# Third pass of a scan, attention and feed-forward kernel: the second y half added by a DMA, y normalized on GpSimd

## The chip, the cores and the metric

The kernel runs on one core of a Trainium2 chip. The metric is the device time of one execution in microseconds (us). The engines are named as the profile names them: PE (TensorE, with PEld for its weight loads), DVE (VectorE), ACT (ScalarE), POOL (GpSimd) and SP (SyncE, which here only issues DMAs). A DMA can be issued from SP's, ACT's or POOL's queue.

## What is computed

Eight images of 64x64 tokens with 96 channels go through two layers. The first is a selective scan in four directions (rows and columns, forwards and backwards), whose four results are added, normalized over 192 channels, gated and projected back to 96 channels. The second is linear attention and a quantized feed-forward block, each behind a layer normalization.

```python
x = x + _L0_conv_ref(_gn(x), ...)
#   y = out_y[:, 0] + inv_y[:, 0] + wh_y + invwh_y          # four directions
#   y = (y - mu) * rsqrt(var + 1e-05) * ln_gamma + ln_beta  # over 192 channels
#   out = (y * silu(z)) @ out_proj_w.T
t = _to_tokens(x)
t = t + _L1_attn_ref(_ln_t(t), ...)      # no softmax: q (k^T v)
t = t + _L1_ffn_ref(_ln_t(t), ...)       # fp8 products, relu, fp8 products
```

## The kernel before

The kernel has three passes. `pass1` normalizes, projects and convolves; `pass2` runs the scans and takes most of the time; `pass3` does everything from the sum of the directions to the output. The change lies in `pass3` alone.

`pass2` leaves two arrays per image in memory, `y_d[b][0]` (the two row directions, added) and `y_d[b][1]` (the two column directions, added), each of 4096 tokens by 192 channels in fp32. `pass3` works on units of 512 tokens (`GRP`), eight per image (`UNITS`), 64 in all. A unit is held as a tile of 128 partitions by 4 groups of tokens (`NU`).

For each unit there are three generators:

- `load(b, q)` (L1139): SP issues five DMAs: `y` and `yo` (the two halves, 384 KB each), two for `zs` (the gate), and `xr` (the residual input). There are five buffers of each (`LOADED`, slots "loaded").
- `first_part(b, q)` (L1154): POOL adds `yo` to `y` (L1162). `standardize` (L1121) takes DVE's statistics of `y` (four `bn_stats`, four `bn_aggr`), ACT's square root, DVE's reciprocal and product, and then four ACT activations, which write the normalized `y` in place (L1137). PE transposes `y`, ACT scales by gamma and beta into `gt`, POOL multiplies `gt` by `zs` (L1179, twice per unit), PE projects, DVE adds the residual into `t`, `t` is standardized into `ln`, and PE adds to the Gram matrix of the image and makes the transposed `lnT`.
- `second_part(b, q)` (L1241): after `attention(b)`, which needs all eight Gram contributions of the image: PE's product with `weff`, DVE's addition, a third standardization (`lf`), transposes, the quantized feed-forward block (with POOL's cast to `hq`, L1278, and POOL's two additions, L1290 and L1291), and the store of `t` by SP.

`fills()` (L1100) writes constants into the padding of `ln` and `lf` once, on POOL; `first_part` waits for it before the second standardization.

The order of instructions on each engine is fixed when the program is written. `weave` (L169) is a planner: each generator yields (engine, cost, delay, slots), and `weave` always takes the step that can begin first on its engine, by costs in us and delays that stand in the code; ties go by rank. First parts have their rank lowered by 12, so they come ahead of second parts. A generator can also yield a key and wait until `done` has it. `room` says how many generators of a kind are open at once: five first parts, five second parts and one load. The next load is opened when the one before has ended. `InOrder` (L85) then ties each engine's instructions to this order. So an instruction whose data is late holds back all that stand behind it on its engine, whatever the plan thought.

In a load, SP's step has a cost of 7.0 (0.0 for the first three units) and a delay of 2.5. It is the load's only step:

```python
end = yield "sp", 0.0 if b == 0 and q < EARLY else 7.0, 2.5, slots["loaded"]
```

Of the kernel before, what the change touches and what calls it, by code (L numbers as in the profile page):

```python
# [33 lines left out]
F32 = mybir.dt.float32  # L34
# [4 lines left out]
ALU = mybir.AluOpType  # L39
# [3 lines left out]
P = 128  # L43
NB, HH, WW, C = 8, 64, 64, 96
L = HH * WW
DI, N, R, K = 192, 16, 6, 4
# [975 lines left out]
def pass3(ctx, tc, g, ident, mhalf, engines, y_d, z_d, out):  # L1022
    nc = tc.nc
    pe, dve, act, pool = engines
    CA = C + 1
    sp = InOrder(tc, nc.sync)

    def pool_of(name, **kwargs):
        return ctx.enter_context(tc.tile_pool(name=f"p3{name}", reuse_waits="tile", bufs=1, **kwargs))

    OPEN = 5
    NU = GRP // P
    UNITS = L // GRP
    LOADED, HELD, EARLY = 5, 20, 3
    first_w, loaded = pool_of("first"), pool_of("loaded")
    wp, one, each, gates, held = (pool_of(name) for name in ("w", "one", "each", "gates", "held"))
    two = ctx.enter_context(tc.tile_pool(name="p3two", reuse_waits="tile", bufs=2))
    banks = {"tr": 3, "mm": 2, "ph": 2}
    slots = {name: Buffers(count) for name, count in {**banks, "loaded": LOADED, "held": HELD, "gates": 3}.items()}
# [59 lines left out]

    def fills():  # L1100

        yield "added", 1
        end = yield "pool", 3.2
        for i in range(OPEN):
            pool.memset(lns[i][:, :, C:P], 0.0)
            pool.memset(lns[i][:, :, C:CA], 1.0)
        for i in range(OPEN):
            pool.memset(lfs[i][:, :, C:P], 0.0)
        done[("filled",)] = end

    done, counts = {}, {}
    loads, holds, grams, weffs = {}, {}, {}, {}

    def take(name, shape):
        which = slots[name].taken
        return pools[name].tile(shape, F32, name=name, tag=f"{name}{which}"), which

    def tokens(src, q):
        return src[q * GRP : (q + 1) * GRP].rearrange("(n p) c -> p n c", p=P)

    def standardize(src, dst, name, cost, which):  # L1121

        yield "dve", 4 * (cost - 0.18) + 0.27
        st = each.tile([P, NU, 6], F32, name=f"st{name}", tag=f"st{name}{which % OPEN}")
        mv = mvs[name][which % OPEN]
        for i in range(NU):
            dve.bn_stats(st[:, i, :], src[:, i, :])
        for i in range(NU):
            dve.bn_aggr(mv[:, i, 0:2], st[:, i, :])
        yield "act", 0.2, 0.2  # L1130
        act.activation(mv[:, :, 1], mv[:, :, 1], AF.Sqrt, bias=eps)
        yield "dve", 0.3, 0.2
        dve.reciprocal(mv[:, :, 1], mv[:, :, 1])
        dve.tensor_reduce(mv[:, :, 3], mv[:, :, 0:3], mybir.AxisListType.X, ALU.mult)
        yield "act", 4 * cost
        for i in range(NU):
            act.activation(dst[:, i, 0 : src.shape[2]], src[:, i, :], AF.Identity, bias=mv[:, i, 3:4], scale=mv[:, i, 1:2])  # L1137

    def load(b, q):  # L1139
        cols = slice(q * GRP, (q + 1) * GRP)  # L1140
        end = yield "sp", 0.0 if b == 0 and q < EARLY else 7.0, 2.5, slots["loaded"]
        of = slots["loaded"].taken
        y, yo = (loaded.tile([P, NU, DI], F32, name=name, tag=f"{name}{of}") for name in ("y", "yo"))
        for o, dst in enumerate((y, yo)):
            sp.dma_start(dst, tokens(y_d[b][o], q))
        zs = loaded.tile([P, 2, GRP], F32, name="zs", tag=f"zs{of}")
        sp.dma_start(zs[:, 0, :], z_d[b][0:P, cols])
        sp.dma_start(zs[:, 1, :], z_d[b][DI - P : DI, cols])
        xr = loaded.tile([P, NU, C], F32, name="xr", tag=f"xr{of}")
        sp.dma_start(xr, tokens(g["x"][b], q))  # L1150
        loads[b, q] = y, yo, zs, xr, of
        done["load", b, q] = end

    def first_part(b, q):  # L1154
        yield "load", b, q
        y, yo, zs, xr, of_loads = loads[b, q]
        end = yield "pool", 1.8, 0.2, slots["held"]
        of_hold = slots["held"].taken
        t = held.tile([P, NU, C], F32, name="t", tag=f"t{of_hold}")
        lnT = held.tile([P, GRP], F32, name="lnT", tag=f"lnT{of_hold}")  # L1160
        holds[b, q] = t, lnT, of_hold
        pool.tensor_add(y, y, yo)  # L1162
        done["added", b * UNITS + q] = end
        if b * UNITS + q < OPEN:
            yield ("gamma",)
        yield from standardize(y, y, "y", 0.44, b * UNITS + q)
        for i, ch in enumerate((slice(0, P), slice(DI - P, DI))):
            yield "pe", 0.6, 0.2, slots["tr"]
            pt, slot = take("tr", [P, GRP])
            for n in range(NU):  # L1170
                pe.transpose(pt[:, n * P : (n + 1) * P], y[:, n, ch], ident)
            end = yield ("act", 0.67) if i else ("act", 0.67, 0.2, slots["gates"])
            if i == 0:
                of_gt = slots["gates"].taken
                gt = gates.tile([P, 2, GRP], F32, name="gt", tag=f"gt{of_gt}")
            act.activation(gt[:, i, :], pt, AF.Identity, bias=gb[:, i, 1:2], scale=gb[:, i, 0:1])
            slots["tr"].release(slot, end)
            yield "pool", 1.23
            pool.tensor_mul(gt[:, i, :], gt[:, i, :], zs[:, i, :])  # L1179
        end = yield "pe", 1.7, 0.2, slots["mm"]  # L1180
        slots["gates"].release(of_gt, end)
        po, slot = take("mm", [P, NU, C])
        for i in range(NU):
            blk = slice(i * P, (i + 1) * P)
            pe.matmul(po[:, i, :], gt[:, 0, blk], w_out0, start=True, stop=False)
            pe.matmul(po[:, i, :], gt[:, 1, blk], w_out1, start=False, stop=True)
        end = yield "dve", 0.55, 0.0
        dve.tensor_add(t, po, xr)
        slots["mm"].release(slot, end)
        slots["loaded"].release(of_loads, end)  # L1190
        ln = lns[(b * UNITS + q) % OPEN]
        yield ("filled",)
        yield from standardize(t, ln, "t", 0.36, b * UNITS + q)
        if b > 0:
            yield "gram", b - 1
        end = yield "pe", 0.9
        if b not in grams:
            grams[b] = ps_one.tile([P, CA], F32, name="pg")
        counts["gram", b] = counts.get(("gram", b), 0) + 1
        for i in range(NU):  # L1200
            first, last = counts["gram", b] == 1 and i == 0, counts["gram", b] == UNITS and i == NU - 1
            pe.matmul(grams[b], ln[:, i, :], ln[:, i, 0:CA], start=first, stop=last)
        if counts["gram", b] == UNITS:
            done["grams", b] = end
        yield "pe", 0.7, 0.2, slots["tr"]
        pl, slot = take("tr", [P, GRP])
        for i in range(NU):
            pe.transpose(pl[:, i * P : (i + 1) * P], ln[:, i, :], ident)
        end = yield "act", 0.47
        act.copy(lnT, pl)  # L1210
        slots["tr"].release(slot, end)
# [29 lines left out]
    def second_part(b, q):  # L1241
# [11 lines left out]
        slots["mm"].release(slot, end)  # L1253
        lf = lfs[(b * UNITS + q) % OPEN]
        yield from standardize(t, lf, "f", 0.36, b * UNITS + q)

        yield "pe", 0.7, 0.2, slots["tr"]
# [36 lines left out]
        slots["held"].release(of_hold, end)  # L1294

    units = [("parameters", -20, parameters()), ("fills", -20, fills())]
    for b in range(NB):
        units += [("first", b * UNITS + q - 12, first_part(b, q)) for q in range(UNITS)]
        units += [("load", b * UNITS + q, load(b, q)) for q in range(UNITS)]
        units.append(("attention", 0, attention(b)))  # L1300
        units += [("second", b * UNITS + q, second_part(b, q)) for q in range(UNITS)]
# [46 lines left out]
```

## Time and profile before

| What | Value |
|---|---|
| time, median of 3 runs | 9698.91 us (9694.32 to 9705.02) |
| profiled execution: time, span | 9701.46 us, 9699.7 us |
| TensorE clock granted, mean | 0.978 |
| busy share of the span: PE, DVE, ACT, POOL | 82%, 96%, 94%, 92% |
| first sum of `y` and `yo` on POOL | begins at 9029.8 us |
| last sum of `y` and `yo` on POOL | begins at 9596.6 us |

The shares of the span are set by `pass2`, which takes most of it. `pass3` is about the last 690 us: its first load is issued at 9006.3 us. In a table of stretches, each row is one stretch of the span with the busy time and the number of instructions of each engine. A group row gives count, busy time and the mean duration of one, then the engine's idle time just before and what ended it. Nearly every instruction is recorded on one line of the code (L93, the helper `InOrder`), so groups are told apart by the names of the tiles they write and read. All `y` tiles of the three passes share the name `y` in the profile.

### The profile page before, as it was taken

Reading aid. Unit: us, or ns where it says so; the run is one execution under the profiler, and the core shown is the slowest. Engines: PE = TensorE matmul, PEld = TensorE weight load, DVE = VectorE, ACT = ScalarE, POOL = GpSimd, SP = SyncE. Lnnn points to the kernel's source line nnn. Section 1 sums busy time; section 2 is a strip of 40 time slices with the busy share of each in tenths; the row PEclk is TensorE's granted clock in tenths of the full one; section 3 lists DMA queues with packets and bytes.
Section 4 is the critical chain, followed back from the end, with each engine's and each line's share of the span. In section 5 each row is a group of like instructions: output and inputs, shape, how many; then the busy total and the mean of one; then the engine's idle time right before and its main releaser. Section 6 shows DMA issues by size and latency. Waiting matters only on the chain.

```text
span 9699.7 us, 163458 instructions
## 1 busy us (share of the span) xinstructions
PE 7931.9 (82%) x57287; PEld 6133.9 (63%) x57287; DVE 9295.1 (96%) x6986; ACT 9091.7 (94%) x21482; POOL 8951.6 (92%) x2903
## 2 busy tenths in 40 slices
PE   8768888888888888888888888888888888888787
PEld 4346666666666666666666666666666666666676
DVE  8989999999999999999999999999999999999688
ACT  6679999999999999999999999999999999999787
POOL 1449999999999999999999999999999999999787
PEclk9889999999999999999999999999999999999898
DMA  6777777799987776799977777899867767999763
GB/s 186 223 222 229 236 233 232 241 221 209 215 225 228 235 228 225 234 215 211 218 226 232 231 227 227 227 208 214 225 220 235 226 219 232 217 209 213 198 184 111
DMA packets 939733, 2120.78 MB, mean 219 GB/s; under 512 B 277707, under 2 KB 425964, under 8 KB 937378
## 3 DMA queue, kind: packets, MB, share of 16 engines
q1 hardware_dynamic: 932226, 2083.33, 77.8%
q10 hardware_dynamic: 6256, 26.05, 0.9%
q8 instruction: 458, 7.50, 0.3%
q14 instruction: 361, 2.96, 0.1%
q0 software_dynamic: 432, 0.94, 0.0%
HBM read 1934.36 MB, written 175.66 MB: 218 GB/s over the span
## 4 chain that ended last, share of the span: by engine, by line
ACT 21%; DVE 13%; issue 9%; POOL 6%; PE 4%; DMA 2%; SPq 0%; DVEq 0%; POOLq 0%; ACTq 0%
DVE h L93 10%; ACT x L93 9%; ACT da L93 7%; POOL c L93 5%; PE wide L93 2%; DVE wide L93 2%; PE acc L93 1%; DMA c<-xd_d 1%; ACT y L93 1%; ACT L93 1%; PE mm L93 1%; POOL xg L93 1%; ACT delta L93 1%; ACT duT L93 1%; ACT lf L93 0%
## 5 line engine op out<-in xcount | busy, mean ns | idle before, releaser
L93 POOL TENSOR_TENSOR c<-c,h 128x2048 f32<-128x2048 f32 x1536 | 6969.2, 4575 | 54.5 <-DVE h L93 38.7
L93 DVE TENSOR_TENSOR_SCAN h<-da,carry,wide 128x1024 f32<-128x1024 f32 x2304 | 5243.3, 2327 | 71.2 <-PE wide L93 33.2
L93 ACT ACTIVATE x<-duT,bT 128x128 f32<-128x128 f32 (+1 forms) x14336 | 4229.9, 368 | 2.1
L93 ACT ACTIVATE da<-delta,a_neg 128x1024 f32<-128x1024 f32 x3072 | 3503.8, 1145 | 178.2 <-DVE h L93 168.1
L93 PE MATMUL acc<-ident,c 128*128 128x128 f32 x24576 | 3126.1, 276 | 360.2 <-POOL c L93 349.1
L93 PEld LDWEIGHTS acc<-ident,c 128*128 128x128 f32 x24576 | 2754.7, 142 | 816.4 <-POOL c L93 703.7
L93 PE MATMUL wide<-ident,x 128*128 128x128 f32 x11264 | 1499.3, 277 | 401.1 <-DVE h L93 314.3
L93 DVE TENSOR_TENSOR_SCAN h<-da,wide 128x1024 f32<-128x1024 f32 x768 | 1704.3, 2267 | 41.5 <-PE wide L93 18.2
L93 PEld LDWEIGHTS wide<-ident,x 128*128 128x128 f32 x11264 | 1250.8, 142 | 662.3 <-ACT x L93 203.9
L93 DVE TENSOR_TENSOR wide<-du,wide 128x1024 f32<-128x1024 f32 x1216 | 1455.0, 1208 | 34.8 <-PE wide L93 31.4
L93 PE MATMUL acc<-sel,zero 96*128 96x512 bf16 x4135 | 1136.6, 380 | 0.0
L93 PE MATMUL wide<-xb,sel 96*128 96x512 bf16 x2432 | 720.4, 380 | 286.3 <-DVE h L93 250.2
L93 POOL TENSOR_TENSOR xg<-duT,bT 128x512 f32<-128x512 f32 (+1 forms) x640 | 901.3, 1428 | 8.1 <-ACT duT L93 8.0
L93 PE MATMUL wide<-ident,xg 128*128 128x128 f32 x3584 | 482.7, 278 | 168.4 <-DVE h L93 153.3
L93 PEld LDWEIGHTS <-zero 96*128 96x128 bf16 x4135 | 401.8, 98 | 320.0 <-issue 4.2
L93 PEld LDWEIGHTS wide<-ident,xg 128*128 128x128 f32 x3584 | 399.5, 143 | 261.6 <-issue 198.5
L93 PEld LDWEIGHTS <-sel 96*128 96x128 bf16 x2432 | 222.6, 98 | 477.3 <-issue 297.0
L93 POOL TENSOR_TENSOR du<-delta,u 128x1024 f32<-128x1024 f32 x192 | 460.9, 2400 | 28.6 <-DMA u<-u_d 25.4
L93 DVE SCALAR_TENSOR_TENSOR u<-xpad,conv_w,u 128x4096 f32<-128x4096 f32 (+1 forms) x104 | 448.3, 4310 | 2.2
L93 ACT ACT_TABLE_LOAD x197 | 252.8, 1283 | 29.4 <-DVE ut L93 13.8
L93 PE MATMUL wide<-ident,du 128*128 128x128 f32 x1536 | 204.8, 276 | 84.6 <-DVE h L93 71.7
L93 PE MATMUL px<-u,w_xp 128*128 128x512 f32 x448 | 225.6, 646 | 49.1 <-ACT u L93 30.3
(148 smaller groups left out, 6016.8 us busy)
## 6 DMA issues: line engine op xcount, KB each, us to landing
c<-xd_d SPq DMA_DIRECT2D x1024, 1024.0 KB
c<-xd_d SPq DMA_DIRECT2D x1024, 512.0 KB
u<-u_d SPq DMA_DIRECT2D x127, 512.0 KB
xdt<-dt_d SPq DMA_DIRECT2D x1146, 36.0 KB
xb<-b_d SPq DMA_DIRECT2D x382, 96.0 KB
u<-u_d SPq DMA_DIRECT2D x128, 256.0 KB
zs<-z_d SPq DMA_DIRECT2D x128, 256.0 KB
y_d<-y SPq DMA_DIRECT2D x96, 256.0 KB
```

Of the source, the lines that this page charges most:

```text
L93: ins = getattr(self.engine, op)(*args, **kwargs).ins
```

## The change

The tile `yo` and its load from SP's queue are gone. In its place POOL's queue issues a DMA that adds `y_d[b][1]` to `y` in SBUF as it lands. This is a second step of the load's generator, with a cost of 0.7 and a delay of 3.0, so a load ends there. POOL's sum is gone. The normalization of `y` is moved from ACT to POOL: four `tensor_scalar` instructions of 192 elements (multiply, then add, with a value per partition each), in one step with a cost of 1.3. `fills` waits for the second load in place of the second sum. The slot "held" is taken by DVE's statistics step instead of POOL's sum. The number of buffers is the same.

```diff
     def fills():
-        yield "added", 1
+        yield "load", 0, 1

     def standardize(src, dst, name, cost, which):
-        yield "dve", 4 * (cost - 0.18) + 0.27
+        if cost is not None:
+            yield "dve", 4 * (cost - 0.18) + 0.27
...
         dve.tensor_reduce(mv[:, :, 3], mv[:, :, 0:3], mybir.AxisListType.X, ALU.mult)
+        if cost is None:
+            yield "pool", 1.3
+            for i in range(NU):
+                pool.tensor_scalar(dst[:, i, :], src[:, i, :], mv[:, i, 1:2], mv[:, i, 3:4], ALU.mult, ALU.add)
+            return
         yield "act", 4 * cost

     def load(b, q):
...
-        y, yo = (loaded.tile([P, NU, DI], F32, name=name, tag=f"{name}{of}") for name in ("y", "yo"))
-        for o, dst in enumerate((y, yo)):
-            sp.dma_start(dst, tokens(y_d[b][o], q))
+        y = loaded.tile([P, NU, DI], F32, name="y", tag=f"y{of}")
+        sp.dma_start(y, tokens(y_d[b][0], q))
...
-        loads[b, q] = y, yo, zs, xr, of
+        loads[b, q] = y, zs, xr, of
+        end = yield "pool", 0.7, 3.0
+        pool.dma_start(y, tokens(y_d[b][1], q), accum_op=ALU.add)
         done["load", b, q] = end

     def first_part(b, q):
         yield "load", b, q
-        y, yo, zs, xr, of_loads = loads[b, q]
-        end = yield "pool", 1.8, 0.2, slots["held"]
+        y, zs, xr, of_loads = loads[b, q]
+        yield "dve", 4 * (0.44 - 0.18) + 0.27, 0.2, slots["held"]
...
-        pool.tensor_add(y, y, yo)
-        done["added", b * UNITS + q] = end
+        yield from standardize(y, y, "y", None, b * UNITS + q)
         if b * UNITS + q < OPEN:
             yield ("gamma",)
-        yield from standardize(y, y, "y", 0.44, b * UNITS + q)
```

## The prediction

> **What bounds the kernel now.** The change is confined to the third pass, so I cut that pass out first. The moments come from the timeline: the first sum of the two y halves starts at 9029.8 us, the last at 9596.6, the span ends at 9699.7. The table of stretches gives the load of the engines in the three stages that this makes (columns: stretch, length, busy time and count of PE, PEld, DVE, ACT, POOL, granted clock, DMA share, GB/s).
>
> ```profile
> 9030.00:9150.00 120.00, 84.59 (x536) 74.83 (x537) 63.62 (x361) 81.31 (x188) 64.32 (x58) 0.77 0.76 224
> 9150.00:9597.00 447.00, 375.57 (x3021) 323.83 (x3020) 383.76 (x1791) 404.54 (x1000) 354.95 (x285) 0.94 0.60 178
> 9597.00:9700.00 103.00, 73.52 (x558) 54.50 (x556) 73.41 (x299) 65.75 (x162) 62.51 (x57) 0.83 0.12 34
> ```
>
> The same table for the tile yo counts 16 sums in stage A (first row) and 48 in stage B. So a unit of 512 tokens costs 120/16 = 7.5 us in A, where no engine is full, and 447/48 = 9.31 us in B. In B, ACT is busy 8.43 us of it (90.5%), DVE 8.00, PE 7.82, POOL 7.39. ACT is the fullest, but DVE is close behind: if ACT shrinks, DVE allows little. The tail of 103 us holds no first parts and isn't touched.
>
> Next, the groups of ACT and POOL for what moves, and rows near to what is new on POOL (columns: count, busy us, mean ns of one, idle before).
>
> ```profile
> L93 ACT ACTIVATE y<-y,mvy 128x192 f32<-128x192 f32 x256 | 119.2, 543 | 17.0 <-DVE mvy L93 15.8 <-DVE mvt L93 1.0 <-DVE mvf L93 0.2
> ```
>
> ```profile
> L93 POOL TENSOR_TENSOR y<-y,yo 128x768 f32<-128x768 f32 x64 | 116.1, 1816 | 18.2 <-DMA yo<-y_d 18.2
> L93 POOL CAST hq<-h 128x1536 fp8e5<-128x1536 f16 x64 | 93.7, 1465 | 55.6 <-DVE h L93 47.1 <-PE ph L93 4.5 <-DMA zs<-z_d 1.8
> ...
> L93 POOL DMA_DIRECT2D xdt<-dt_d x6 | 3.2, 548 | 0.0
> ...
> L93 POOL DMA_DIRECT2D u<-u_d x1 | 0.6, 577 | 0.0
> ...
> masks.py:199 POOL TENSOR_SCALAR_AFFINE_SELECT ident<-ident 128x128 f32<-128x128 f32 x1 | 0.3, 288 | 0.0
> ```
>
> The loads' times to landing stand in the chain of waits (start, us, what) and, for POOL's queue, in the list of DMA issues (last number).
>
> ```profile
> 9037.09 4.13 DMA yo<-y_d
> ...
> 9053.36 4.00 DMA yo<-y_d
> ...
> 9070.17 7.49 DMA y<-y_d
> ...
> 9198.26 3.28 DMA y<-y_d
> ```
>
> ```profile
> u<-u_d POOLq DMA_DIRECT2D x1, 512.0 KB, 12.1
> ...
> xdt<-dt_d POOLq DMA_DIRECT2D x6, 36.0 KB, 8.2
> ```
>
> Last, DVE's timeline for one unit's statistics in B, from their start to the last reduction.
>
> ```profile
> 9296.25 1.13 DVE L93 BATCH_NORM_STATS2 sty<-y 128x6 f32<-128x192 f32 x4
> ...
> 9299.20 0.17 DVE L93 RECIPROCAL mvy<-mvy 128x4 f32<-128x4 f32 x1
> 9299.41 0.17 DVE L93 TENSOR_REDUCE mvy<-mvy 128x4 f32<-128x12 f32 x1
> ```
>
> That is 9299.58 - 9296.25 = 3.3 us, ACT's square root and its queue included. The same stretch in A, 9079.20 to 9081.40, takes 2.2 us.
>
> **The change part by part.** *Off ACT:* four normalizations, 119.2/64 = 1.86 us a unit; ACT falls to 6.6 us in B. Alone this is worth at most what DVE leaves: 63 us of DVE idle time in B.
>
> *On POOL:* the sum goes, 1.82 us. Four normalizations of 192 elements come, which no row shows. From below: the cast does 1536 elements in 1.465 us, so 768 take 0.73, plus three more starts of about 0.1 (the mean of the 128x4 memset): 1.0 us. From above: the two-input sum of 768 elements, 1.82, plus the same starts: 2.1. The one-input AFFINE_SELECT of 128 elements took 0.288; four of them with 1.5 times the elements are 1.15 to 1.73. It is nearest in kind; I take 1.4. The issue of the adding load: 0.548 to 0.577 us for 18 to 128 rows; this one has 512 runs of 768 bytes, so from 0.52 (the xb loads) to 4 x 0.577 = 2.3. Rows of 18 and 128 hardly differ, so 0.7. POOL in B: 7.39 - 1.82 + 0.7 + 1.4 = 7.7 us, not the bound; with both upper ends 10.0, and then it is.
>
> *SP* issues four loads a unit instead of five, about 0.5 us less of a queue that waits for buffers anyway: nothing. *DMA:* the bytes from memory are the same; the destination is read as well, on engines 60% busy in B: nothing but the landing time below. *DVE* keeps its work. *The memsets* of fills, 2.3 us on POOL, now wait for the second load instead of the second sum; POOL's waits of 9.7 and 3.8 us there hide them, without that they cost 2.3 us once.
>
> *The new wait.* The adding load waits on POOL for the first y load, and everything on POOL waits behind it. That y has one planned period of lead (7.0 + 2.5 us), against 3.3 to 7.5 to land, so this wait is nothing; in a burst, up to 7.5 once. The wait that costs is the next: DVE's statistics for the landing, and behind them all of DVE's queue.
>
> *What the order does.* The planner opens one load at a time (room 1). So far a load ended with SP's step, and the next could start at once. Now it ends with POOL's step, so the next load begins on SP no earlier than the adding load of this unit, and its own adding load comes at least 7.0 + 2.5 = 9.5 planned us later. In the plan the normalization of this unit follows its adding load by 0.7 + 3.0 + 1.61 + 0.4 + 0.5 = 6.2 us. So POOL's queue reads: adding load u, normalization u, adding load u+1. The queue is fixed, and on the chip it is a loop with one unit in it: landing, statistics, square root, reciprocal, normalization, next adding load. Its length is a floor for the period, and two-unit prefetch, which today lets five loads run ahead of the sum, no longer hides the second half.
>
> Landing time L, from POOL's issue: below, the fastest row of the same 384 KB, 3.28; above, POOL's own transfers, 12.1. Its twin yo took 4.0 to 4.1, y in a burst 7.5. The adding load also reads its destination and starts beside the next unit's y, zs and xr loads. I take 5.0. The loop in B: 5.0 + 3.3 + 1.4 + 0.2 (two releases) = 9.9; in A: 5.0 + 2.2 + 1.4 + 0.2 = 8.8.
>
> Sum: A 16 x (8.8 - 7.5) = +21; B 48 x (9.9 - 9.31) = +28; the first unit waits 5.0 instead of 1.8, +3. Together +52 on the profiled execution's 9701.5 us, which is 2.5 above the median of the runs: 9751, so 9750. The loop is level with today at L = 4.2 (64 L = 48 x 4.41 + 16 x 3.7).
>
> The Trainium skill, "DMA: Bandwidth & Descriptors", section "Anatomy of one DMA — SWDGE (gpsimd) path", gives a POOL-issued transfer about 2.0 us plus its bytes at 436 GB/s; as an estimate 2.9 us here. The loads above took longer than that, but by it the loop would be 7.8 us and the change a gain of the second rival's size.
>
> A second rule speaks against the change, and a row bears on it.
>
> ```profile
> L93 DVE TENSOR_SCALAR h<-h,b1q x144: 319/346/1909, 9153.0 to 9599.5; 128x512 f16<-128x512 f16 x144
> ```
>
> DVE's bias step on h takes 346 ns in the median and up to 1909 (columns minimum/median/maximum). The Trainium skill, "SBUF — State Buffer", section "Who interferes with whom", says that such an operation and GpSimd lock each other out of a shared port pair, and a descriptor write waits too. Three medians, 1.0 us, before an issue would make L 6.0 and the sum about 64 us more; shorter POOL instructions would, by the same rule, give DVE some back.
>
> **The rivals.** *1, the other side: ACT's relief comes through.* If L stays below 4.2, the loop is shorter than today's period and DVE becomes the bound. For it: yo's 4.0 to 4.1, and ACT's 90.5%. Against: POOL's rows of 8.2 and 12.1. Price: DVE at ACT's share today, 8.00/0.905 = 8.84 us, gives 48 x -0.47 = -23; DVE at 95%, 8.4, gives -44. Middle: -35, 9665.
>
> *2: POOL becomes the bound* (issue 2.3, normalization 2.1). For it: 512 runs where the rows have 128 at most. Against: 18 rows cost nearly what 128 do. At 10.0 us busy and 90.5%, B's period is 11.0: 48 x 1.7 = +82; A's loop 9.5: 16 x 2.0 = +32; +3: about 9815.
>
> *3: both cancel*: L near 4.2 and DVE's queue takes what ACT gave. 9699.
>
> **How the numbers follow.** Measurements of this kernel tell about 0.2% (19 us) from no change. The forecast (the loop) gets 0.50: 0.47 of it slower, 0.03 within. Rival 1 gets 0.28: 0.26 faster, 0.02 within. Rival 2 gets 0.12, all slower. Rival 3 gets 0.10: 0.09 within, 0.01 faster. So faster 0.27, same 0.14, slower 0.59. The likeliest case's own range is L from 4.5 to 6.2: 9718 to 9830. The whole range goes down to rival 1 with DVE near 95%, 9660, and up to L of 6.5, 9850; L of 7.5 (9911) and the joint upper ends lie outside.
>
> **What would show it.** Right: DVE idle before the y statistics, released by a DMA of y, some 1 us a unit; ACT near 70% in B; adding loads on POOL 9.5 to 10.5 us apart, each behind the previous unit's normalization. Rival 1: no such wait, DVE above 90%, period below 9. Rival 2: POOL above 90%, issues above 1.5 us or normalizations above 0.5 each. The prediction is wrong if the landing is under 4 us, or if POOL's queue holds the next adding load ahead of the normalization.

## The result and the profile after

The changed kernel takes 9961.58 us (median of 4 runs, 9958.64 to 9964.67) against 9698.66 for the kernel before (4 runs, 9694.32 to 9705.02): a ratio of 1.0271, 95% interval 1.0253 to 1.0288. It is slower by 263 us, five times the 52 us of the forecast, and far outside its range.

All of it is in the third pass. The table of stretches of the changed kernel, with the same columns as before (length, busy time and count of PE, PEld, DVE, ACT, POOL, granted clock, DMA share, GB/s):

```profile
9030.00:9150.00 120.00, 75.69 (x393) 62.32 (x391) 38.53 (x213) 39.35 (x85) 66.16 (x88) 0.72 0.66 150
9150.00:9850.00 700.00, 493.17 (x3290) 421.53 (x3288) 428.52 (x1965) 365.45 (x880) 452.79 (x510) 0.79 0.53 123
9850.00:9960.00 110.00, 77.28 (x463) 57.80 (x461) 64.65 (x255) 53.23 (x126) 58.72 (x61) 0.73 0.17 36
```

The middle stage has grown from 447 to 700 us, and no engine is full in it: PE 70%, POOL 65%, DVE 61%, ACT 52%. The tail has hardly changed (110 us). So nothing has become a bound by its work; each unit simply takes longer. From the first to the last statistics of y (9050.4 to 9877.7 us) there are 63 steps of 13.1 us; before it was 8.9 (9039.4 to 9602.9). The 4.2 us more, 63 times, are the whole loss.

What the new instructions cost on POOL, in its groups:

```profile
L93 POOL TENSOR_SCALAR y<-y,mvy 128x192 f32<-128x192 f32 x256 | 125.7, 499 | 135.4 <-DVE mvy L93 105.0 <-DVE mvt L93 27.7 <-DVE mvf L93 2.5
L93 POOL DMA_DIRECT2D y<-y_d x64 | 80.9, 1285 | 0.0
```

A normalization of four groups is 1.96 us (125.7/64), a little more than the sum it came with (1.82), and an issue is 1.3 us in the mean, more than twice what the rows of before showed. The tile view of y and the list of waits of DVE tell the rest:

```profile
DMA to landing us min/median/max: 5.0/5.7/8.8
```

```profile
DVE sty L93 <- DMA y<-y_d: 156.3, 52, 8.9
DVE t L93 <- PE mm L93: 103.1, 50, 5.7
```

DVE stands 156 us in 52 waits at the statistics of y for a landing (before: 21.8 us, for POOL's sum). A second wait has grown from 39.3 to 103.1 us: DVE's addition of the residual waits for PE, not for a landing. The length of a wait doesn't tell by itself whether it costs time; the experiments have to.

The loop of the prediction is plainest in the first stage, where only first parts run. POOL's timeline (start, length, what; in brackets the idle time before it):

```profile
9073.77 1.21 POOL L93 DMA_DIRECT2D y<-y_d  x1
9078.58 1.26 POOL L93 TENSOR_TENSOR gt<-gt,zs 128x512 f32<-128x512 f32 x1 [3.60 <-ACT gt L93]
9083.83 1.27 POOL L93 TENSOR_TENSOR gt<-gt,zs 128x512 f32<-128x512 f32 x1 [3.99 <-ACT gt L93]
9085.08 1.95 POOL L93 TENSOR_SCALAR y<-y,mvy 128x192 f32<-128x192 f32 x4
9086.98 1.22 POOL L93 DMA_DIRECT2D y<-y_d  x1
```

One adding load, the unit's normalization, the next adding load: 13.2 us, of which POOL does nothing for 7.6. DVE's timeline shows what lies between:

```profile
9079.83 1.14 DVE L93 BATCH_NORM_STATS2 sty<-y 128x6 f32<-128x192 f32 x4 [1.01 <-DMA y<-y_d]
9080.89 0.36 DVE L93 BATCH_NORM_AGGREGATE mvy<-sty 128x2 f32<-128x6 f32 x4
...
9084.46 0.18 DVE L93 RECIPROCAL mvy<-mvy 128x4 f32<-128x4 f32 x1 [2.95 <-ACT mvy L93]
9084.67 0.17 DVE L93 TENSOR_REDUCE mvy<-mvy 128x4 f32<-128x12 f32 x1
```

Landing 6.1 us, statistics to last reduction 5.0, normalization and its start 2.1. The middle piece was 2.2 us in the stage A of before. Here ACT's square root has to wait its turn behind three steps of other units (9081.55 to 9084.12 on ACT), because the order says so. In the next round it is the landing: the chain of waits has the next adding load at 8.84 us.

```profile
9086.98 8.84 DMA y<-y_d
```

The loop holds in the whole pass. In 62 of the 64 units POOL's queue has the unit's normalization ahead of the next adding load, and the statistics begin 0.1 us after the landing in the mean. The means of the pieces, from the starts, ends and landings in the trace, a round being the time from the issue of one adding load to the next (A: rounds 4 to 10, B: rounds 11 to 63):

| Piece of the round | Taken in the prediction, us | Measured in A, us | Measured in B, us |
|---|---|---|---|
| landing, from the issue | 5.0 | 6.37 | 6.42 |
| statistics to the last reduction | 2.2 in A, 3.3 in B | 2.58 | 2.98 |
| normalization | 1.4 | 1.95 | 1.97 |
| between landing and statistics | | 0.02 | 0.11 |
| between last reduction and normalization | | 0.69 | 0.65 |
| between normalization and next issue | | 0.72 | 1.55 |
| the three pieces between, together | 0.2 | 1.43 | 2.31 |
| round | 8.8 in A, 9.9 in B | 12.3 | 13.7 |

In B, POOL is busy for 2.1 of the 2.2 us that lie before and after the normalization. Its instructions there belong to other units (sums and casts of second parts, products with the gate); they stand in its queue between the pieces of the loop.

### The profile page after: what moved, and what is told of

It is laid out like the page before. It is cut to its first block, busy times and chain, and to the rows that moved or that the text cites. A ratio compares the mean times of both kernels' runs of the same rounds, so it can differ in the third digit from the quotient of the medians.

```text
span 9960.3 us, 163555 instructions
## 1 busy us (share of the span) xinstructions
PE 8048.9 (81%) x57287; PEld 6226.2 (63%) x57287; DVE 9304.3 (93%) x6986; ACT 8998.4 (90%) x21226; POOL 9039.6 (91%) x3159
## 4 chain that ended last, share of the span: by engine, by line
ACT 18%; DVE 13%; issue 10%; POOL 7%; DMA 5%; PE 4%; SPq 0%; DVEq 0%; POOLq 0%; ACTq 0%
DVE h L93 10%; ACT x L93 8%; ACT da L93 7%; POOL c L93 4%; DMA y<-y_d 2%; DVE wide L93 2%; PE wide L93 2%; DMA c<-xd_d 1%; PE acc L93 1%; POOL y L93 1%; PE mm L93 1%; ACT L93 1%; ACT delta L93 1%; ACT duT L93 1%; POOL gt L93 1%
```

## The experiments

Twelve kernels were run. Times are compared with runs of the kernel before that were made beside them on the same chip, so the difference is given with each. "Period" is the time from the first to the last statistics of y over 63. The text calls an order *spaced* where the plan has the loads at least 9.5 us apart (one load open, whose two steps take 7.0 + 2.5 us), and any other *open*.

| Run | Order | Adding load | Normalization | Against before, us | Ratio, 95% interval | Period, us |
|---|---|---|---|---|---|---|
| changed kernel | spaced | yes | POOL | +263 | 1.0253 to 1.0288 | 13.1 |
| e1_add_only | spaced | yes | ACT | +150 | 1.0142 to 1.0172 | 11.5 |
| e2_norm_only | before's | no | POOL | +45 | 1.0033 to 1.0063 | 9.7 |
| e3_room3 | open | yes | POOL | +83 | 1.0072 to 1.0103 | 10.2 |
| e4_plain | spaced | plain load | POOL | +168 | 1.0156 to 1.0190 | 11.9 |
| e5_sp_cost | open | yes | POOL | +84 | 1.0069 to 1.0099 | 10.2 |
| e6_true | spaced, other costs | yes | POOL | +209 | 1.0202 to 1.0233 | 12.3 |
| e7_true_room5 | open | yes | POOL | +58 | 1.0047 to 1.0077 | 9.7 |
| e8_add_true_room5 | open | yes | ACT | +13 | 1.0004 to 1.0023 | 9.0 |
| e9_split | open | yes | half, half | +33 | 1.0021 to 1.0047 | 9.4 |
| e10_before_spaced | spaced | no | ACT | +94 | 1.0081 to 1.0114 | 10.7 |
| e11_add_six | open, six buffers | yes | ACT | -10 | 0.9979 to 0.9998 | 8.7 |
| e12_norm_spaced | spaced | no | POOL | +204 | 1.0199 to 1.0236 | 12.4 |

The 9.5 us are a least distance. How long a plan is can be worked out without a chip, by running `weave` alone over the generators of `pass3`; the order that it gives for POOL is the order in the traces. The planned step from one unit's y statistics to the next, taken as the period in the table, is 8.5 us in the kernel before and 10.6 in the changed kernel: 2.1 us a unit, half of the loss, stand in the plan before any instruction is late. It is 10.2 in e10, 9.9 in e1, 11.6 in e12 and 12.4 in e6, but 8.4 in e2 and e3, 8.5 in e5 and e11, 8.6 in e8, 8.8 in e9 and 9.2 in e7.

### One part alone: e1_add_only, e2_norm_only

```diff
 # e1: the changed kernel, normalization back on ACT
         if cost is None:
-            yield "pool", 1.3
-            for i in range(NU):
-                pool.tensor_scalar(...)
-            return
+            cost = 0.44
```

> The adding load stays on POOL, the normalization of y goes back to ACT. Loop theory (landing, statistics, normalization and the next adding load form one chain on POOL's queue, 13.1 us a unit in the changed kernel): POOL's queue no longer holds the normalization in front of the next adding load, so the chain opens; the period falls to 9.5 to 11 us and the time to 9720 to 9830. Rival A (POOL's added work, 1.24 us of issue and 1.97 us of normalization a unit, sets the period): 1.97 us less per unit of 13.1, 64 x 2.0 = 126 us less, near 9835. Rival B (the transfer itself, or descriptors held up by DVE, is what is slow): no change, 9930 or more.

Measured 9860.87, 150 more than before and some 113 less than the changed kernel. It lies above what the loop theory gave and nearest to rival A, and so settled neither. With the normalization on ACT, the landing still holds DVE's queue (102.7 us in 40 waits) and the period is 11.5 us. The chain of waits in the middle of the stage:

```profile
9304.52 9.27 DMA y<-y_d
...
9313.82 1.14 DVE sty L93 x4
...
9316.16 5.26 PE mm L93 x24
...
9328.73 1.27 POOL gt L93
...
9331.76 8.31 DMA y<-y_d
```

A loop is there still, but through other engines: landing, statistics, then what stands behind them in DVE's queue, PE, ACT, POOL's product with the gate, the next adding load. So in this kernel, whose adding loads no longer wait for a normalization, it is not the normalization that closes the loop.

```diff
 # e2: the kernel before, in standardize
+        if name == "y":
+            yield "pool", 1.3
+            for i in range(NU):
+                pool.tensor_scalar(dst[:, i, :], src[:, i, :], mv[:, i, 1:2], mv[:, i, 3:4], ALU.mult, ALU.add)
+            return
         yield "act", 4 * cost
```

> From the kernel before, only the normalization of y is moved to POOL; both halves are loaded by SP and POOL adds them. Loop theory: no transfer stands in the chain, so only POOL's sum counts, 7.39 + 1.97 = 9.4 us a unit against 9.31 before: 9.7 to 10.2 us a unit, 9715 to 9760. Rival A (POOL's work sets the period): this kernel has more work on POOL than the changed one (1.82 for the sum against 1.24 for the issue), so 9930 to 10000. Rival B: as before or faster, 9660 to 9700.

Measured 9755.41, +45, as the loop theory had it. POOL is now the fullest engine (stretch 9150 to 9550):

```profile
9150.00:9550.00 400.00, 319.66 (x2469) 279.83 (x2469) 337.21 (x1472) 270.37 (x658) 364.63 (x388) 0.90 0.57 166
```

POOL 91%, DVE 84%, ACT 68%. In an order without the spacing, moving the normalization trades one full engine for another and loses a little. Rival A, that POOL's work alone makes 260 us, is refuted: this kernel has more work on POOL than the changed one.

### The order alone: e3_room3, e5_sp_cost

```diff
 # e3
-    weave(units, {"parameters": 1, "fills": 1, "load": 1, "first": OPEN, ...
+    weave(units, {"parameters": 1, "fills": 1, "load": 3, "first": OPEN, ...
 # e5
-        end = yield "sp", 0.0 if b == 0 and q < EARLY else 7.0, 2.5, slots["loaded"]
+        end = yield "sp", 0.0 if b == 0 and q < EARLY else 3.0, 2.5, slots["loaded"]
```

> The changed kernel with one number different: the planner may have three loads open instead of one. The work is the same, only the order of the queues differs, so that adding loads can be issued ahead of the normalization of the unit before. Loop theory: the chain opens and POOL's sum of work (7.39 - 1.82 + 1.24 + 1.97 = 8.8 us) or DVE (8.0 us) bounds the period: 9.2 to 9.9 us, 9690 to 9770. Rival A and rival B, for which order does not matter: 9900 or more.

> The changed kernel with SP's step of a load planned at 3.0 instead of 7.0; one load open, old costs of the adding load. The planned distance of two adding loads falls from 9.5 us or more to 5.5 or more, so the plan is no longer set by the loads. If the distance in the plan is what costs: near the run with three open loads (9793), 9770 to 9830. If it must be a second open load: 9900 or more.

Measured 9793.30 (+83) and 9786.15 (+84). e3 is a little above its range, e5 in it. Each is one number in the planner's tables, no instruction differs, and each takes some 180 of the 263 us away. It need not be a second open load: with one load open, a planned distance of 5.5 instead of 9.5 us does the same. What costs is the order that comes of loads so far apart in the plan. The two runs change two things at once: the plan is shorter (8.4 and 8.5 us a unit against 10.6), and the loop is opened, for the next adding load stands ahead of the unit's normalization in 41 and 43 of the 64 units. So they show that the order is the cause, not which of the two does it. In e3, the engines are fuller throughout:

```profile
9150.00:9550.00 400.00, 310.16 (x2376) 273.92 (x2375) 313.98 (x1423) 261.50 (x635) 329.31 (x370) 0.89 0.71 160
```

Against 280, 246, 211 and 259 us of PE, DVE, ACT and POOL in the same stretch of the changed kernel.

### The landing: e4_plain

```diff
-        pool.dma_start(y, tokens(y_d[b][1], q), accum_op=ALU.add)
+        pool.dma_start(y, tokens(y_d[b][1], q))
```

> The changed kernel with a plain load on POOL's queue in place of the adding one: the second half overwrites the first in the tile, so the first half is left out of the output. Order, waits and bytes from memory are the same; the destination is not read. If the addition makes the landing long (median 5.7 us from issue to landing with it, against 4.0 to 4.1 for SP's load of the same half before), the landing falls to 4 to 4.5 us and the time by 64 x 1.2 to 1.7 = 77 to 109 us, to 9850 to 9885. If the queue makes it long: landing 5.5 us or more and 9930 to 9965.

Measured 9879.03, +168: some 95 us less than with the addition. The time lies in the first range, the landing between the two. Its tile view of y, issue and landing:

```profile
L93 POOL DMA_DIRECT2D y<-y_d x61: 797/802/952, 9056.7 to 9789.4; - x61
...
DMA to landing us min/median/max: 3.6/4.9/8.1
```

Against 1152/1242/2252 ns and 5.0/5.7/8.8 us with the addition. So the addition makes the issue 0.44 us longer, which is part of the landing (it is counted from the start of the issue), and the median landing 0.8 us. In the mean of all 64 the landing is 6.4 us with the addition and 4.9 without: 1.5 us, times 64 some 96, about the 95. In the changed kernel the landing goes with what SP issues beside it. The chain of waits (first four lines) and SP's timeline:

```profile
9302.87 8.40 DMA y<-y_d
...
9320.44 8.05 DMA y<-y_d
...
9399.90 6.08 DMA y<-y_d
...
9411.58 5.89 DMA y<-y_d
```

```profile
9303.44 0.45 SPq L93 DMA_DIRECT2D y<-y_d  x1
...
9319.78 0.45 SPq L93 DMA_DIRECT2D y<-y_d  x1
```

```profile
9397.63 0.44 SPq L93 DMA_DIRECT2D y<-y_d  x1
...
9408.32 0.45 SPq L93 DMA_DIRECT2D y<-y_d  x1
```

When SP issues the next unit's y, zs and xr within 0.7 us of the adding load, it takes 8.0 to 8.4 us; when they went out 2.3 and 3.3 us earlier, 5.9 to 6.1. Over all 64 adding loads it is much the same: 19 were issued within 0.7 us of SP's issue of a y load and landed in 8.4 us in the median (5.7 to 8.8), the other 45 in 5.3 (5.0 to 8.8). Without the addition it is 5.3 for 20 loads and 4.4 for 44. So the company goes with 3.1 us more when the load adds, and with 0.9 when it doesn't. No run moved SP's loads by themselves.

### The planner told the measured costs: e6_true, e7_true_room5

```diff
 # e6
-        end = yield "pool", 0.7, 3.0
+        end = yield "pool", 1.25, 6.0
...
-            yield "pool", 1.3
+            yield "pool", 2.0
 # e7: as e6, and
-    weave(units, {..., "load": 1, ...
+    weave(units, {..., "load": 5, ...
```

> The changed kernel with the planner told what was measured: issue 1.25 (was 0.7), landing delay 6.0 (was 3.0), normalization 2.0 (was 1.3); still one load open at a time. The same instructions, another order. Loop theory: in the plan the normalization now follows its adding load by 1.25 + 6.0 + 1.6 + 0.9 = 9.75 us, later than the earliest next adding load at 9.5, so the next adding load mostly comes ahead of it, and DVE's queue no longer stands 2 to 5 us at the statistics: the chain opens without a second load in the plan; 9730 to 9830. If only the number of open loads mattered: 9920 or more. Rival B (the transfer itself is what costs): 9900 or more.

Measured 9915.78, +209. The loop theory's 9730 to 9830 missed by far. In this order the next adding load does stand ahead of the normalization for 39 of the 64 units, and DVE's wait for landings has fallen from 156 to 66.5 us, yet the period is 12.3 us. So the chain that I had named was opened for most units and little came back. But the edit did a second thing: with one load open, the larger costs also made the plan longer, 12.4 us a unit against 10.6, and the chip ran at 12.3. So this run doesn't tell what opening the loop alone is worth. The number of open loads was a poor name for it too, as e5 shows.

> The same measured costs and five loads open in the plan. Loop theory: neither wait is left; POOL's work (8.8 us a unit) is the bound, at 95 to 100% of it 8.8 to 9.3 us a unit: 9670 to 9740, at least 50 us below the run with three open loads and the old costs (9793). If POOL's issue or DVE's hold on descriptor writes costs more than the rows show: 9790 or more.

Measured 9764.74, +58: between the two ranges. Against e3 (+83), the right costs and a wider plan bring another 25 us; DVE's wait for landings is down to 31.4 us. What is left is about what the normalization costs by itself (e2).

### The spacing without the adding load: e10_before_spaced, e12_norm_spaced

```diff
 # e10: the kernel before, in load
         loads[b, q] = y, yo, zs, xr, of
+        end = yield "pool", 0.7, 3.0
         done["load", b, q] = end
```

The added step issues nothing; it only makes the planner believe in it.

> The kernel before, with both halves loaded by SP, POOL's sum and ACT's normalization; only the planner is given the second step of the changed load (POOL, cost 0.7, delay 3.0) with no instruction in it. So the plan's loads are as far apart as in the changed kernel, and no adding load exists. If the order alone (spaced loads in a one-unit plan) costs the time: 9840 or more. If the adding load's landing must stand in the chain for it: 9700 to 9750. In between, the share of each is read from it.

Measured 9796.68, +94: between the two. The same instructions as the kernel before, SP's loads and POOL's sum included, and 1% slower:

```profile
9150.00:9550.00 400.00, 314.92 (x2284) 266.15 (x2284) 297.06 (x1352) 311.86 (x755) 271.62 (x218) 0.88 0.51 153
```

Every engine has room (PE 79%, ACT 78%, DVE 74%, POOL 68%), and POOL's sums hardly wait for a transfer (4.7 us). Two waits have grown: POOL's product for ACT's scaling (119.9 us, 60.4 before) and DVE's residual for PE (89.7 us, 39.3 before). The first is 92.9 us in e11 too, which loses nothing. The traces tell more by the units under way at once, from the start of a unit's y statistics to the end of its copy into `lnT`, in the mean of the stretch 9150 to 9550: 4.2 before, 2.5 in e10 and 2.1 in the changed kernel, but 3.5 in e3 and 4.4 in e11.

e12 is e10 with the edit of e2.

> The kernel before with the empty second step in the plan of a load (as in the run that spaced the loads without an adding load, 9797) and the normalization of y on POOL; SP loads both halves and POOL adds them. It is the last cell of the table of three parts: spaced order, adding load, normalization on POOL. If the normalization costs in the spaced order what it costs in the open one (49 us): 9835 to 9860, and then some 50 of the changed kernel's 259 us come only when landing and normalization stand in one chain. If the parts simply add (normalization 100 us in the spaced order, 9961 less 9861): 9885 to 9910.

Measured 9913.79, +204, just above the range of "the parts simply add". In the spaced order the normalization on POOL costs 204 - 94 = 110 us; in the open one 45.

This completes a table of three parts. In the spaced order: spacing alone 94, adding load 150 - 94 = 56 more, normalization 110 more; the sum is 260, and the changed kernel has 263. In the open order: normalization 45 (e2), adding load 13 (e8), sum 58, and the run with both has 58 (e7). The parts add in each order, and the spacing is a price by itself and makes the two others dearer by 108 us together. e7 and e8 have five open loads and measured costs, e2 the order of before; the open corner isn't one single order. That the parts add doesn't make them three separate waits: in the changed kernel the round is the one loop. Part of what the normalization costs in the spaced order stands in the plan, which it lengthens from 10.2 to 11.6 us a unit there (e10 to e12), and not at all in the open one (8.5 before, 8.4 in e2).

### Is there a faster version: e8_add_true_room5, e9_split, e11_add_six

```diff
 # e8: e7 with the normalization on ACT
 # e9: e8 with groups 0 and 1 normalized on POOL, 2 and 3 on ACT
 # e11: e8 with six buffers, six open loads and a landing of 8.0
-    LOADED, HELD, EARLY = 5, 20, 3
+    LOADED, HELD, EARLY = 6, 20, 3
...
-        end = yield "pool", 1.25, 6.0
+        end = yield "pool", 1.25, 8.0
```

> The adding load alone (normalization on ACT, as before), with the measured costs and five loads open. Loop theory: ACT is the bound as in the kernel before (8.43 us a unit), POOL has 0.57 us less than before: 9670 to 9710, no change against before, 150 us or more below the adding load alone with the old order (9861). If the adding load as such costs: 9800 or more.

Measured 9719.59, +13, a little above its range: the adding load costs next to nothing when the plan lets it run ahead. Its landings are no shorter for it: 6.5 us in the median, against 5.7 in the changed kernel.

> The adding load with measured costs and five loads open, and the normalization shared: two of the four groups on POOL, two on ACT. Work a unit: POOL 7.39 - 1.82 + 1.24 + 0.98 = 7.8, ACT 8.43 - 0.93 = 7.5, DVE 8.0. Loop theory: nothing above 8.0, the period falls to 8.5 to 9.0, 9640 to 9690: faster than the kernel before. If the transfers' share or the longer first part costs more: 9700 to 9760.

Measured 9740.18, +33: the second of its ranges. Although no engine is above 82% in the stretch from 9150 to 9550, sharing the normalization is slower than leaving it on ACT. Why stays open. POOL's wait for the statistics (42.4 us) is new against e8; its wait for ACT's scaling is smaller instead (48.8 us, 102.7 in e8).

> The adding load alone (normalization on ACT) with six buffers of loads instead of five (the second half's tile is gone, so they fit), six loads open in the plan, issue 1.25 and a landing delay of 8.0. If DVE's remaining wait for landings (25 us) and the plan's tightness are what is left: 9670 to 9705. If ACT is the bound, as in the kernel before: 9705 to 9730.

Measured 9692.88 (9678.06 to 9702.50, 10 runs) against 9702.58: 10 us less, a ratio of 0.9979 to 0.9998. That is the first of its ranges, and DVE's wait for landings fell from 25.0 us in e8 to 4.3. It is the one run not slower than the kernel before, by about 0.1%, and there ACT is the full engine again:

```profile
9150.00:9550.00 400.00, 337.81 (x2788) 290.38 (x2786) 350.12 (x1658) 371.33 (x919) 303.54 (x262) 0.97 0.83 189
```

The sixth buffer, the longer planned landing and the sixth open load were not taken apart.

## Why the prediction was wrong

**What held.** The side: slower. The place: the one open load in the planner, whose load now ends with POOL's step, so that planned loads lie 9.5 us or more apart. e3 and e5 show that the order is the cause of most of the loss: one number undoes some 180 of 263 us. The loop of landing, statistics, normalization and next adding load is there in 62 of 64 units. ACT's relief brought nothing (rival 1), and POOL did not become the bound (rival 2: it is 65% busy). The signs named under "What would show it" came on the forecast's side but larger: DVE waits 2.4 us a unit for landings (156 us over 64 units, some 1 us foretold), and ACT is at 52% (near 70% foretold).

**The step that failed** is the sum of the loop: "The loop in B: 5.0 + 3.3 + 1.4 + 0.2 (two releases) = 9.9; in A: 5.0 + 2.2 + 1.4 + 0.2 = 8.8." Measured it is 13.7 and 12.3. The landing was 6.4 instead of 5.0, the normalization 2.0 instead of 1.4, and the pieces between were 2.3 us in B and 1.4 in A instead of 0.2. That last term was put at nothing but releases because POOL's queue was read as "adding load u, normalization u, adding load u+1", as if nothing of other units stood between; nearly all of it is POOL's work for them. With the measured rounds, the prediction's own sum is 16 x (12.3 - 7.5) + 48 x (13.7 - 9.31) = 288 us, against 263 measured. So the form held for the changed kernel, and the sizes were wrong.

The second fault is "Its length is a floor for the period": there is another floor under it. The spacing was given a price through this one loop alone, and all that it does to the other queues was put at nothing. e10 measures that by itself: 94 us with no adding load in the program, more than the whole forecast of 52. The plan's distance was treated as slack that the chip would press out, since SP's real step is some 2.5 us and not 7.0. It wasn't: the chip ran the order, with 2.1 to 2.5 units under way at once instead of 4.2. It fits this that taking the normalization out of the loop (e1) gave back only 113 of the 263 us.

**The terms, one by one**, nearly all off to the same side:

- The landing L: taken as 5.0; 6.4 in the mean and 5.7 in the median. Of the mean the addition is 1.5 (e4), and the long landings, 8.4, are those with SP's loads beside them. SP's store, which waits for POOL's last addition of an older unit, lets those loads go at the same time as the adding load that stands next on POOL; I had named them as company and given them no term of their own.
- The issue (POOL's work, and part of the landing): 0.7 taken, 1.24 measured in the median. That 18 and 128 rows cost nearly the same did not carry to 512 rows with an addition; 0.80 without it.
- The normalization: 1.4 taken, 1.96 measured; the upper bound by the sum's row (2.1) was the near one. Four short instructions of 0.49 us cost more than one sum of all 768 elements.
- The statistics to the last reduction: 2.2 taken in A and 3.3 in B; 2.6 and 3.0 in the mean, up to 5.0 in the round shown, where ACT's queue holds the square root.

Three slips in the working change little: by the estimate of 2.9 us the change would be a gain of the first rival's size, not the second's; the tail does hold the end of the last first parts, since the last sum begins at 9596.6; and the 1.61 for the statistics' step is 1.51 by the code (1.31 + 0.2).

**The rules of the Trainium skill.** "DMA: Bandwidth & Descriptors", section "Anatomy of one DMA — SWDGE (gpsimd) path", gave an estimate of 2.9 us for the transfer; the runs have 5.0 at the least with the addition and 3.6 without. "SBUF — State Buffer", section "Who interferes with whom", would have descriptor writes wait for DVE's bias step; the 15 issues that ran beside such a step took 1.23 to 1.34 us, the other 49 1.23 in the median, so no such wait shows in them, and the bias step itself took 588 ns in the mean against 612 before.

**Open.** Why each part costs two to four times as much in the spaced order as in the open one (110 against 45 us, 56 against 13) is only in part answered, by the lengths of the plans. How the 263 us divide between the loop and the longer plan isn't shown: no run opened the loop and left the plan as long as it was. The granted clock (below) may have a share.

## What to carry to other kernels

A planner that orders queues by hand-set costs is part of the kernel: a step added at the end of a generator whose kind may be open only once lengthens the planned distance of all that follow, and the chip did not undo it here. After such a change, work out the period of the units in the plan itself and hold it against that of before (here 10.6 against 8.5 us), and try more open ones of that kind. Measured costs alone don't mend such a plan: with one load open they made it longer (e6). A queue that closes a loop also holds the work of other units between its pieces; it has to be in the sum. To tell an order's price from that of its instructions, give the planner the step without the instruction, and the instruction without the distance.

## What the runs showed that was not expected

The granted clock of PE in the stretch from 9150 to 9550 us goes with how busy the pass keeps it: 0.97 in e11, 0.94 in the kernel before, 0.88 in e10, 0.80 in the changed kernel. The projection's matmuls take 286 ns in the mean at 0.97 and 0.94, 311 at 0.88 and 323 at 0.80. The stretch of the kernel before and of the changed one, and the group of PE in the changed one:

```profile
9150.00:9550.00 400.00, 336.61 (x2688) 289.03 (x2687) 341.94 (x1598) 361.23 (x893) 316.46 (x253) 0.94 0.61 181
```

```profile
9150.00:9550.00 400.00, 280.16 (x1909) 241.60 (x1907) 245.98 (x1142) 211.28 (x510) 259.49 (x291) 0.80 0.53 122
```

```profile
L93 PE MATMUL mm<-w_out,gt 128*128 128x96 f32 x480 | 76.8, 323 | 6.4 <-POOL gt L93 6.0
```

So among these four kernels, the ones that wait more also compute more slowly. The Trainium skill, "TensorE: Matmul & The Clock Gate", section "Part 1: The HAM clock gate", says that the clock is granted by recent activity, which agrees; how much of the 263 us it makes was not tried.

On POOL, the issues got longer with the number of rows and with the addition: 0.55 us for 18 rows of 2 KB, 0.58 for 128 rows of 4 KB, 0.80 for 512 rows of 768 bytes, 1.24 for the same with the addition.
